# A four-layer graph network on one Trainium2 core: the planner of the order gives each DMA a time on one lane

## The chip, the cores and the metric

The kernel runs on one core of a Trainium2 chip. The core has five engines with an instruction queue each: TensorE (PE: matrix products), VectorE (DVE), ScalarE (ACT), GpSimd (POOL) and SyncE (SP, which here does nothing but issue DMAs). Each engine works its queue in the order of the program and waits on semaphores for what other engines and transfers make. The metric is the device time of one execution in microseconds.

## What is computed

128 graphs of 128 nodes with 512 features each go through four attention layers. Each is wrapped in a residual and a normalisation:

```python
x = _layernorm(x + _L0_gnn_ref(x, adj, ...))   # scores of one head; mixes x itself
x = _layernorm(x + _L1_gnn_ref(adj, x, ...))   # x @ W1 (512 x 1024), 4 heads, elu, @ W2 (1024 x 512), 1 head
x = _layernorm(x + _L2_gnn_ref(x, adj, ...))   # 8 heads of 64 columns
x = _layernorm(x + _L3_gnn_ref(x, adj, ...))   # one head; mixes x itself, elu
```

An attention layer adds a source score of a node i and a target score of a node j, takes a leaky relu, masks by the adjacency matrix, takes a softmax over one side, and multiplies by the features. In layer 1 and 2 the features are projected first. All is float32.

## The kernel before

**One graph's work.** `graph(g)` builds the list of operations of one graph. Each is an `Op`: an engine, a planned cost, a function that emits the instructions, and the buffers that it reads and writes. The helpers that matter here:

- `spread` (line 569) takes a column of scores and makes a matrix whose rows are all that column: VectorE transposes 32 x 32 blocks (L578), one DMA writes the row to a scratch in DRAM (L581, `row<-sT`), a second reads it back broadcast to 128 partitions (L585, `w<-row`). Five times a graph: three with one row, one with four, one with eight.
- `turned` (line 591) transposes n blocks of 128 x 128: VectorE transposes within 32 x 32 blocks (L596), a DMA writes the tile to scratch (L601, `scr<-w`), and a second reads it back with the blocks in their places. That read is L611 (`w<-scr`, in pieces of 128 bytes), or L606 for a matrix that is the moving side of a product. Eight times a graph: five with n = 4 and three with n = 1; L606 takes one of each, L611 the other six.
- `attend` (line 626) does the leaky relu (L635, ScalarE), mask and row minimum (L643, VectorE), the exponential (L652, ScalarE) and then `turned`. `norm` (line 667) is the normalisation; `project` (line 698) the product with a weight (L704); `mixed` (L719) the product of attention and features. `halves` (line 743) does the second product of layer 1 for two graphs together (L788) with seven block products in the place of eight.

A graph so issues 30 DMAs on SP's queue: 5 rows, 5 broadcasts, 8 writes to scratch, 8 reads back, and x, twice the adjacency matrix, and the store.

**How the order comes about.** The Python program plans before it emits anything:

1. `plan` (line 78) places one graph's operations in a period of 28 us so that, repeated for each next graph, no engine is taken twice. It uses the latencies of `LATENCY`. The result is a due time for each operation of each graph.
2. `order` (line 144) takes all operations of all graphs and of the set-up by due time and plays the run through. It keeps a clock for each engine, a time at which each operation's inputs are there (`ready`), and a time at which each buffer comes free (`released`). At each step it takes, over the engines, the operation that can start first; on one engine the oldest due one that can start at once. None may be more than 30 us (`AHEAD`) of due time ahead of the oldest that is still open. What comes out is the order of each engine's queue, and the place that each buffer takes. After an operation that starts at t, its readers may start at t + cost + `extra` + the engine's latency in `FLOW`. For SP that latency is 4.5 us, whatever else is under way.

So the planned times never reach the chip. The chip sees the order, the places and the semaphores.

**Set-up.** `at` (line 295) adds operations with due times of their own, `load` (line 307) the weights' DMAs on the queues of ACT, SP and POOL, with an `extra` of kb / 190. For w1s (16 loads) the program says 256 KB each, and 128 KB are moved; for w2s (4 loads) it says 600, and 512 are moved.

Of the kernel before, what the change touches and what calls it, by code (L numbers as in the profile page):

```python
# [29 lines left out]

PERIOD = 28.0
LATENCY = {"PE": (0.0, 0.8), "DVE": (0.15, 1.6), "ACT": (0.1, 1.6), "POOL": (0.1, 1.6), "SP": (6.8, 6.8)}
FLOW = {"PE": (0.0, 0.6), "DVE": (0.15, 0.9), "ACT": (0.1, 0.9), "POOL": (0.1, 0.9), "SP": (4.5, 4.5)}
AHEAD = 30.0
URGENCY = 0.3
BANKS = 8
# [22 lines left out]


class Op:
    def __init__(self, engine, cost, emit, ins, outs, extra, uses=()):
        self.engine, self.cost, self.emit, self.extra = engine, cost, emit, extra
        self.wait = 0
        self.ins, self.outs = ins, outs
        self.uses = list(uses)
        self.bufs = list(dict.fromkeys([*ins, *outs, *uses]))

    def done(self, reader=None, latency=None):
        own, other = (latency or LATENCY)[self.engine]  # L70
        return self.cost + self.extra + (own if reader is self.engine else other)


class Pipeline:
# [69 lines left out]
    def order(self, events):  # L144

        ops, n = [e[3] for e in events], len(events)
        ends, first, last, readers, open_uses = {}, {}, {}, {}, {}
        before, after = [0] * n, [[] for _ in ops]
        makes, coming = [[] for _ in ops], {}
        for i, op in enumerate(ops):  # L150
            need = {last[b] for b in op.ins + op.uses if b in last}
            for b in op.outs:
                need.update([last[b]] if b in last else [], readers.get(b, ()))
                if b not in first:
                    first[b] = events[i][0]
                    if b.tag != "const":
                        makes[i].append(b)
                        coming.setdefault(b.tag, []).append(i)
            need.discard(i)
            before[i] = len(need)  # L160
            for q in need:
                after[q].append(i)
            for b in op.ins + op.uses:
                readers.setdefault(b, []).append(i)
            for b in op.outs:
                last[b], readers[b] = i, []
            for b in op.bufs:
                open_uses[b] = open_uses.get(b, 0) + 1
                ends[b] = max(ends.get(b, 0.0), events[i][0] + op.done())

        free = {}
        for b, t in first.items():
            if b.tag != "const":
                places = free.setdefault(b.tag, [])
                s = next((s for s, e in enumerate(places) if e <= t), len(places))
                places[s : s + 1] = [ends[b]]
        assert len(free["ps"]) <= BANKS, "too few banks"
        free = {tag: [(0.0, s) for s in range(BANKS if tag == "ps" else len(p))] for tag, p in free.items()}
        ready, released, clock = [0.0] * n, {}, {e: 0.0 for e in FLOW}
        known = {e: [i for i in range(n) if not before[i] and ops[i].engine == e] for e in FLOW}  # L180
        issued, low, out = [False] * n, 0, []

        def start(i):
            t = max(clock[ops[i].engine], ready[i])
            for b in makes[i]:

                rank = 0
                for q in coming[b.tag]:
                    if q >= i or rank >= len(free[b.tag]):
                        break  # L190
                    rank += 1
                if rank >= len(free[b.tag]):
                    return None
                t = max(t, free[b.tag][rank][0])
            return t

        while len(out) < n:
            best = None
            for e, waiting in known.items():
                found = None  # L200
                for i in waiting:
                    if events[i][0] > events[low][0] + AHEAD and i != low:
                        break
                    t = start(i)
                    if t is not None and (found is None or t < found[0]):
                        found = (t, i)
                        if t <= clock[e]:
                            break
                if found and (best is None or found < best):
                    best = found  # L210
            t, i = best
            op = ops[i]
            known[op.engine].remove(i)
            issued[i] = True
            out.append((events[i][1], op))
            for b in makes[i]:
                b.slot = free[b.tag].pop(0)[1]
                coming[b.tag].remove(i)
            clock[op.engine] = t + op.cost
            for q in after[i]:  # L220
                ready[q] = max(ready[q], t + op.done(ops[q].engine, FLOW))
                before[q] -= 1
                if not before[q]:
                    insort(known[ops[q].engine], q)
            for b in op.bufs:
                released[b] = max(released.get(b, 0.0), t + op.done(None, FLOW))
                open_uses[b] -= 1
                if not open_uses[b] and b.slot is not None and b.tag != "const":
                    insort(free[b.tag], (released[b], b.slot))
            while low < n and issued[low]:  # L230
                low += 1
        return out
# [3 lines left out]
def tile_gat_stack(  # L236
# [55 lines left out]
    setup = []  # L292
    queue = {"SP": nc.sync, "ACT": nc.scalar, "POOL": nc.gpsimd}

    def at(t, engine, cost, emit, ins=(), outs=(), extra=0.0):
        setup.append((t, Op(engine, cost, emit, list(ins), list(outs), extra)))

    def mark():

# [256 lines left out]
    def graph(g):  # L556

        ops = []

        def op(engine, cost, emit, ins=(), outs=(), extra=0.0, uses=()):  # L560
            ops.append(Op(engine, cost, emit, list(ins), list(outs), extra, uses))

        def bank():
            return Buf("ps", [P, 512])
# [4 lines left out]
        def spread(col, nh):  # L569


            sT, row = Buf(f"sT{nh}", [P, nh, 32]), Buf(f"row{nh}", [nh, P])

            def turn():
                c, out = col(), sT.ap
                if len(c.shape) > 2:
                    out = out.rearrange("p (a b) c -> p a b c", a=c.shape[1])
                nc.vector.transpose(out, c.unsqueeze(len(c.shape)).to_broadcast([*c.shape, 32]))  # L578

            op("DVE", 0.12 + 0.033 * nh, turn, [col.buf], [sT])  # L580
            op("SP", 0.6, lambda: nc.sync.dma_start(  # L581
                out=row.ap.rearrange("h (b c) -> b h c", b=P // 32), in_=sT.ap[0:P:32]
            ), [sT], [row])
            db = Buf(f"db{nh}", [P, nh, P])
            op("SP", 0.4, lambda: nc.sync.dma_start(  # L585
                out=db.ap.rearrange("p h j -> p (h j)"),
                in_=row.ap.rearrange("h j -> (h j)").partition_broadcast(P),
            ), [row], [db], 1.0 + 0.1 * nh)
            return db

        def turned(src, n, moving=False):
# [8 lines left out]
            ), [src], [zb])  # L600
            op("SP", 0.4, lambda: nc.sync.dma_start(  # L601
                out=scr.ap, in_=zb.ap.rearrange("p b h c -> p (b h c)")
            ), [zb], [scr], 0.2 * n)
            flat = lambda: scr.ap.rearrange("p f -> (p f)")
            if moving:
                op("SP", 0.6, lambda: nc.sync.dma_start(  # L606
                    out=out.ap.rearrange("p h i -> p (h i)").rearrange("p (q e) -> p q e", q=4),
                    in_=flat().rearrange("(q p e) -> p q e", q=4, p=P),
                ), [scr], [out], 1.0)
                return out  # L610
            op("SP", 0.65, lambda: nc.sync.dma_start(  # L611
                out=out.ap.rearrange("p h (q c) -> p h q c", q=4),
                in_=flat().rearrange("(q p h c) -> p h q c", q=4, p=P, h=n),
            ), [scr], [out], 1.5)
            return out

        class Col:
            def __init__(self, buf, a, n):
                self.buf, self.a, self.n = buf, a, n
# [204 lines left out]
        def first(g):  # L824


            x0, at = Buf("x0", [P, F]), Buf("adj", [P, P], I32)
            op("SP", 0.4, lambda: nc.sync.dma_start(out=x0.ap, in_=x[g]), [], [x0], 1.0)
            op("SP", 0.4, lambda: nc.sync.dma_start(out=at.ap, in_=adj[g]), [], [at], 1.0)
            ae = Buf("ae", [P, P], I32)  # L830
            m0, m1, m2 = (Buf(f"m{k}", [P, P]) for k in range(3))
            op("POOL", 0.6, lambda: nc.gpsimd.tensor_tensor(out=ae.ap, in0=at.ap, in1=eye_i, op=ALU.add), [at], [ae])
# [72 lines left out]
        def third(g, st, xl2):  # L905
# [60 lines left out]


            at, m3 = Buf("adj", [P, P], I32), Buf("m3", [P, P])
            op("SP", 0.4, lambda: nc.sync.dma_start(out=at.ap, in_=adj[g]), [z3], [at], 1.0)
            mask(m3, at, ALU.is_equal)  # L970
            db = spread(Col(sc4, 1, 1), 1)
            pt, ri = attend(db, 0, 1, Col(sc4, 0, 1), m3, scaled=True)
# [6 lines left out]

            op("POOL", 1.3, lambda: nc.gpsimd.tensor_add(y.ap, y.ap, x3.ap), [y, x3], [y])  # L980
            norm(y, on_act=True)
            op("SP", 0.4, lambda: nc.sync.dma_start(out=out[g], in_=y.ap), [y], [], 1.0)
        if g == B:

            whole = graph(None)
# [59 lines left out]
```

## Time and profile before

| what | value |
|---|---|
| median of 3 runs | 3286.35 us (3285.72 to 3295.9) |
| the profiled execution | 3273.89 us, its span 3272.1 us |
| granted TensorE clock, mean | 0.975 |
| busy: PE, DVE, POOL, ACT | 94%, 90%, 69%, 66% of the span |
| DMA queue of SP | 598.97 MB, 74.6% of the 16 engines' span |
| packets under 512 bytes | 1311562 of 1657571 |
| stretch 600 to 1000 us: PE, DVE, POOL, ACT busy | 387.45, 370.20, 291.49, 278.45 of 400 us |
| chain that ended last | DVE 32%, PE 24%, DMA 19%, ACT 7%, POOL 6%, issue 6% |

The busy time of an engine is the union of its instructions' spans. For matmuls the ends are modelled. A table of stretches gives for each one the busy us of PE, PEld (weight loads), DVE, ACT and POOL with the number of instructions in brackets, then the granted clock, the share of the DMA engines, and GB/s. A line of waits reads: engine, tile and line that waited, what ended the wait, us in total, times, longest.

### The profile page before, as it was taken

To read this page: it belongs to the slowest core of one execution; us is meant where nothing else is said; L and a number is where in the kernel's file an instruction comes from. 1 tells how busy PE (TensorE), PEld (TensorE's weight loads), DVE (VectorE), ACT (ScalarE), POOL (GpSimd) and SP (SyncE) were. 2 spreads that over 40 slices of the span, in tenths; PEclk is the share of its full clock that TensorE was granted. 3 is DMA by queue.
4 is the path that set the end of the run, shared out by engine and by line. 5 is a ranking of instruction groups with operands and counts; after the bars stand their busy time and mean duration, and the time that the engine had idled before them with its cause. 6 is when DMAs were issued, how large, how long until landed. Compare 5 with 4: busy or idle time off the path is not lost.

```text
span 3272.1 us, 62627 instructions
## 1 busy us (share of the span) xinstructions
PE 3072.9 (94%) x14822; PEld 2483.6 (76%) x14822; DVE 2939.1 (90%) x10185; ACT 2157.7 (66%) x7427; POOL 2259.4 (69%) x3211
## 2 busy tenths in 40 slices
PE   7899999999999999999999999999999999999974
PEld 4688787778777877777888777777877777777852
DVE  6878999999989999998999998999989989999985
ACT  1346677667667666766776766767766667676764
POOL 2556777777777777766777777777777777777654
PEclk7899999999999999999999999999999999999985
DMA  4357778787777787877887777778787777787775
GB/s 114 94 129 188 191 194 193 190 201 191 196 192 193 201 189 193 200 182 185 204 194 193 195 191 200 187 193 203 191 201 190 192 193 191 194 198 195 185 180 124
DMA packets 1657571, 606.13 MB, mean 185 GB/s; under 512 B 1311562, under 2 KB 1508170, under 8 KB 1657204
## 3 DMA queue, kind: packets, MB, share of 16 engines
q1 hardware_dynamic: 1655836, 598.97, 74.6%
q8 instruction: 121, 1.98, 0.2%
q14 instruction: 246, 2.02, 0.2%
q0 software_dynamic: 576, 2.10, 0.2%
q10 hardware_dynamic: 792, 1.06, 0.1%
HBM read 374.43 MB, written 227.48 MB: 184 GB/s over the span
## 4 chain that ended last, share of the span: by engine, by line
DVE 32%; PE 24%; DMA 19%; ACT 7%; POOL 6%; issue 6%; SPq 1%; POOLq 0%; DVEq 0%; ACTq 0%
PE ps L704 14%; DVE w L643 12%; DMA w<-scr 8%; DMA scr<-w 6%; DVE w L596 6%; PE ps L788 5%; DVE st L670 3%; ACT w L652 3%; DMA w<-row 2%; ACT w L635 2%; PE ps L719 2%; DMA w<-in_x_dram 2%; PE ps L932 2%; DVE w L727 2%; PE ps L890 2%
## 5 line engine op out<-in xcount | busy, mean ns | idle before, releaser
L704 PE MATMUL ps<-w1s,w 128*128 128x258 f32 x4096 | 930.6, 385 | 21.7 <-DMA w<-scr 13.1
L652 ACT ACTIVATE w<-w,nm 128x128 f32<-128x128 f32 x1920 | 752.8, 393 | 285.4 <-DVE nm L643 265.8
L704 PEld LDWEIGHTS ps<-w1s,w 128*128 128x128 f32 x4096 | 779.0, 192 | 191.6 <-DVE z L936 18.7
L788 PE MATMUL ps<-w2s,w 128*128 128x257 f32 x3584 | 873.8, 383 | 10.0 <-POOL w L774 9.6
L643 DVE CUSTOM_DVE_ANT_0 w<-w,w 128x128 f32<-128x128 f32 x1920 | 841.2, 538 | 33.5 <-ACT w L635 16.2
L788 PEld LDWEIGHTS ps<-w2s,w 128*128 128x128 f32 x3584 | 657.3, 191 | 122.2 <-issue 27.4
L635 ACT ACTIVATE w<-w,xl 128x128 f32<-128x128 f32 x1536 | 482.1, 389 | 244.7 <-DMA w<-row 240.4
L704 PE MATMUL ps<-wha,w 128*128 128x273 f32 x2048 | 522.5, 402 | 75.6 <-DMA w<-scr 66.5
L596 DVE STREAM_TRANSPOSE w<-w 128x512 f32<-128x512 f32 (+1 forms) x1024 | 538.5, 539 | 37.1 <-POOL w L662 18.6
L704 PEld LDWEIGHTS ps<-wha,w 128*128 128x128 f32 x2048 | 379.1, 193 | 236.3 <-issue 123.1
L674 POOL TENSOR_SCALAR rd<-mv 128x1 f32<-128x1 f32 x512 | 143.0, 279 | 432.2 <-DVE mv L671 310.8
L689 ACT ACTIVATE w<-w,mr,rd 128x512 f32<-128x512 f32 x384 | 311.7, 812 | 140.1 <-POOL mr L682 75.6
L944 POOL TENSOR_TENSOR w<-z,w 128x512 f32<-128x512 f32 x128 | 151.6, 1184 | 342.7 <-DVE z L936 195.1
L675 POOL TENSOR_TENSOR rd<-rd,neghalf 128x1 f32<-128x1 f32 x512 | 345.8, 675 | 42.7
L652 ACT ACTIVATION_READ_ACCUMULATOR w<-w,nm 128x1 f32 x1920 | 362.2, 189 | 0.0
L670 DVE BATCH_NORM_STATS2 st<-w 128x6 f32<-128x512 f32 x512 | 340.3, 674 | 13.1 <-POOL w L980 9.2
L635 ACT ACTIVATE w<-w,sc 128x128 f32<-128x128 f32 x384 | 151.4, 396 | 297.2 <-DMA scr<-w 237.6
L875 POOL TENSOR_TENSOR xl<-xl,b1t 128x512 f32<-128x512 f32 x256 | 322.7, 1282 | 0.0
L719 PE MATMUL ps<-w,w 128*128 128x512 f32 x512 | 273.8, 617 | 36.5 <-DMA w<-scr 26.1
L932 PEld LDWEIGHTS ps<-xl,w 128*128 128x128 f32 x2048 | 263.0, 195 | 39.1 <-issue 11.2
L643 DVE DVE_READ_ACCUMULATOR2_ANT nm<- 128x1 f32 x1920 | 287.2, 150 | 0.0
L932 PE MATMUL ps<-xl,w 128*128 128x66 f32 x2048 | 256.1, 274 | 18.6 <-DMA w<-scr 16.5
(183 smaller groups left out, 4481.3 us busy)
## 6 DMA issues: line engine op xcount, KB each, us to landing
scr<-w SPq DMA_DIRECT2D x640, 256.0 KB
w<-scr SPq DMA_DIRECT2D x640, 256.0 KB
w<-row SPq DMA_DIRECT2D x128, 512.0 KB
w<-in_x_dram SPq DMA_DIRECT2D x128, 256.0 KB
w<-row SPq DMA_DIRECT2D x128, 256.0 KB
out_dram<-w SPq DMA_DIRECT2D x128, 256.0 KB
w<-row SPq DMA_DIRECT2D x384, 64.0 KB
scr<-w SPq DMA_DIRECT2D x384, 64.0 KB
```

The costliest lines, as they stand in the source:

```text
L596: op("DVE", 0.12 + 0.133 * n, lambda: nc.vector.transpose(zb.ap.rearrange("p b h c -> p h b c"), src.ap.rearrange("p (h b c) -> p h b c", ...
L635: nc.scalar.activation(z.ap[:, h, :], db.ap[:, h0 + h, :], AF.Prelu, bias=src(h0 + h), alpha=SLOPE)
L643: nc.vector.tensor_tensor_reduce(out=zz.ap[:, h, :].rearrange("p (b a) -> p a b", b=4), in0=z.ap[:, h, :].rearrange("p (a b) -> p a b", b= ...
L652: nc.scalar.activation(zz.ap[:, h, :], zz.ap[:, h, :], AF.Exp, bias=nm.ap[:, h : h + 1], scale=-1.0, accum_out=rs.ap[:, h : h + 1],)
L670: op("DVE", 0.6, lambda: nc.vector.bn_stats(st.ap, y.ap), [y], [st])
L675: nc.gpsimd.tensor_tensor(out=rd.ap, in0=rd.ap, in1=neghalf, op=ALU.pow)
L689: op("ACT", 0.6, lambda: nc.scalar.activation(y.ap, y.ap, AF.Identity, bias=mr.ap, scale=rd.ap), [y, rd, mr], [y])
L704: op("PE", w * 4 / 2400 + 0.006, lambda k=k: nc.tensor.matmul(px.ap[:, :w], lhsT=lhs.ap[:, k, :], rhs=wa(k, c), start=(k == 0), stop=(k == ...
L719: op("PE", width * 4 / 2400, lambda: nc.tensor.matmul(pa.ap[:, :width] if len(xv.shape) == 2 else pa.ap.rearrange("p (s c) -> p s c", s=2) ...
L788: return lambda: nc.tensor.matmul(q[b].ap[:, :C2], lhsT=x()[:, k, :], rhs=w2s[:, slot, k, :], start=(fresh and k == 0), stop=(k == 3), ski ...
L875: op("POOL", 1.3, lambda nh=nh: nc.gpsimd.tensor_add(xl.ap[:, nh, : 2 * FH], xl.ap[:, nh, : 2 * FH], b1t[:, nh * 2 * FH : (nh + 1) * 2 * F ...
L932: op("PE", 0.225, lambda u=u, h=h: nc.tensor.matmul(pa.ap[:, u * CH : (u + 1) * CH], lhsT=pt.ap[:, u, :], rhs=xl3.ap[:, h * CH : (h + 1) * ...
```

## The change

- `Op` gets a field `dma`: the time for which a transfer holds the lane. Each DMA of a graph is given one, by its kind and its n, and each load of the set-up has its kb / 190 there.
- `order` keeps one more clock, `lane`. A transfer ends at max(lane, end of its issue) + `dma`, and that is the lane's new time. Readers may start 3.2 us after it, on every engine; its buffers come free then too. The term `extra` no longer counts in `order`.
- `FLOW["SP"]` goes from 4.5 to 3.2.
- `plan` and `LATENCY` stay as they are, and so do the `extra` terms there; only set-up operations have none any more. Costs, operations and what they emit stay.

```diff
-FLOW = {..., "SP": (4.5, 4.5)}
+FLOW = {..., "SP": (3.2, 3.2)}
 ...
-    def __init__(self, engine, cost, emit, ins, outs, extra, uses=()):
+    def __init__(self, engine, cost, emit, ins, outs, extra, uses=(), dma=0.0):
+        self.dma = dma
 ...
-        ready, released, clock = [0.0] * n, {}, {e: 0.0 for e in FLOW}
+        ready, released, clock, lane = [0.0] * n, {}, {e: 0.0 for e in FLOW}, 0.0
 ...
-            clock[op.engine] = t + op.cost
+            clock[op.engine] = done = t + op.cost
+            own, other = FLOW[op.engine]
+            if op.dma:
+
+                done = lane = max(lane, done) + op.dma
+                own = other = FLOW["SP"][0]
             for q in after[i]:
-                ready[q] = max(ready[q], t + op.done(ops[q].engine, FLOW))
+                ready[q] = max(ready[q], done + (own if ops[q].engine == op.engine else other))
 ...
             for b in op.bufs:
-                released[b] = max(released.get(b, 0.0), t + op.done(None, FLOW))
+                released[b] = max(released.get(b, 0.0), done + other)
 ...
-    def at(t, engine, cost, emit, ins=(), outs=(), extra=0.0):
-        setup.append((t, Op(engine, cost, emit, list(ins), list(outs), extra)))
+    def at(t, engine, cost, emit, ins=(), outs=(), dma=0.0):
+        setup.append((t, Op(engine, cost, emit, list(ins), list(outs), 0.0, dma=dma)))
 ...
 # the time on the lane, by transfer (cost and extra unchanged)
+ L581 row<-sT                     dma=0.02 + 0.03 * nh
+ L585 w<-row        1.0 + 0.1*nh, dma=0.03 + 0.19 * nh
+ L601 scr<-w             0.2 * n, dma=0.05 + 0.17 * n
+ L606 w<-scr, moving         1.0, dma=0.27 + 0.15 * n
+ L611 w<-scr                 1.5, dma=0.415 * n
+ x in, out                   1.0, dma=0.72
+ adj (twice)                 1.0, dma=0.22
```

## The prediction

> **What bounds the kernel now.** I read the cores' view first (one core, granted clock 0.975, so no second core disturbs), then the page's busy shares, then the busy time by stretches:
>
> ```profile
> PE 3072.9 (94%) x14822; PEld 2483.6 (76%) x14822; DVE 2939.1 (90%) x10185; ACT 2157.7 (66%) x7427; POOL 2259.4 (69%) x3211
> 0.00:100.00 100.00, 74.59 (x194) 45.70 (x195) 69.36 (x258) 13.96 (x42) 28.30 (x43) 0.78 0.41 109
> 200.00:300.00 100.00, 99.04 (x490) 83.19 (x489) 81.50 (x271) 58.59 (x209) 60.66 (x76) 1.00 0.64 162
> 600.00:1000.00 400.00, 387.45 (x1909) 315.93 (x1909) 370.20 (x1299) 278.45 (x970) 291.49 (x414) 1.00 0.79 196
> ```
>
> The steady stretch sets the time. 14822 matmuls over 128 graphs are 115.8 a graph; 1909 of them in 400 us are 16.5 graphs, so a graph takes 24.3 us. TensorE is busy 97% of it, VectorE 93%, the DMA engines 79%. The fill and the tail lose some 160 us (1071 matmuls in the first 300 us are 9.2 graphs, or 224 us at the steady rate), and I expect little change there.
>
> How much is there to win? From runs of matmuls without a break in the chain that ended last:
>
> ```profile
> 1515.78 3.22 PE ps L704 x14
> 1519.00 1.73 PE ps L932 x16
> 1522.53 0.86 PE ps L719 x2
> 1552.99 6.96 PE ps L704 x32
> 1561.25 1.78 PE ps L890 x16
> ```
>
> At these rates a graph needs 6.96 (layer 1 projection) + 28 x 0.2175 = 6.09 (layer 2, from a run of 8 in 1.74 us that the chain has at 186.8 us) + 16 x 0.23 = 3.68 (layer 2 heads' projection on wha) + 3 x 0.86 + 1.73 + 1.78 + 0.11 = 22.9 us. Against 24.3 that leaves 1.4 us a graph: 0.8 us is open idle time (busy sums to 2610 of 2700 us from 300 to 3000), the rest is hidden in matmuls that the model shows as busy.
>
> The waits of TensorE from 300 to 3000 us, and the DMA issue before one of them:
>
> ```profile
> PE ps L704 <- DMA w<-scr: 65.4, 83, 3.0
> PE ps L844 <- POOL w L732: 7.5, 14, 2.0
> PE ps L890 <- DMA w<-scr: 1.7, 4, 0.6
> 1507.45 7.39 SPq L611 DMA_DIRECT2D w<-scr  x3
> 1507.45 7.38 DMA w<-scr
> ```
>
> Columns of a wait: total us, times, longest. So 67 of the 90 us of open idle are waits for one kind of transfer, the read back of a transposed tile (L611). The last two lines show why some are late: three such reads went out in one burst, SP stood in their issue for 7.39 us, and the chain charges 7.38 us to the transfer. The order was laid down with 0.65 + 1.5 + 4.5 = 6.65 us for every such read, alone or third in line. The same chain charges 6.45 and 6.10 us to the next two. I also matched the trace's packets to the issues by size and order: from 300 to 3000 us the last packet of a 2048-packet read lands 3.3 us after its issue at the tenth percentile, 4.75 at the median, 6.1 at the ninetieth. A transfer's time depends on what stands ahead of it, and the kernel's order does not know it.
>
> **What the Trainium skill says.** "DMA: Bandwidth & Descriptors", section Queues, rings and completion order: the queue of one issuing engine is one ring on each DMA engine, consumed in ring order. The burst of three agrees, and so one lane is a fair picture. The same page, Issuing engines are not separate DMA queues: loads from other engines share the 16 DMA engines; the change puts the weights from ACT and POOL on the lane too, and the GB/s row (114 in the first slice) shows no second set of engines. "TensorE: Matmul & The Clock Gate", HAM oscillation: idle gaps of more than about 3.4 us halve the clock. The trace agrees once in the steady part: after 3.0 us of idle at 1540 us, clock 0.50 from 1540.2 to 1543.4 us. "Perfetto Trace Analysis", Identifying the Most-Contended Engine: matmul busy time is a poor measure of the room left; hence the working by rates above.
>
> **The change, part by part.** It adds and removes no instruction; every duration stays, and only the order in each engine's queue and the buffers' places move.
>
> *The read L611 (four of n = 4, two of n = 1 a graph).* Planned from 6.65 to 0.65 + 1.66 + 3.2 = 5.51 us alone, and 1.66 more for each one ahead: third in a burst from 6.65 to some 7.5 (3 x 1.66 of lane, less the 1.3 by which its own issue is later). Against the packets, the old figure is 3.3 us over a lone read (tenth percentile) and 0.5 over the late ones (ninetieth); the new one is 2.2 over the first and 1.4 over the second.
>
> *The other transfers, planned alone, before to after:* score row to DRAM (L581) 5.1 to 3.85; broadcast of one row (L585) 6.0 to 3.82, of four 6.3 to 4.39, of eight 6.7 to 5.15; tile to scratch (L601) 5.7 to 4.33; L606 of four 6.1 to 4.67. Last packets land (median, from issue) at 1.2, 2.9, 3.5, 5.0, 3.2 and 2.9 us. The new figures are nearer and mostly still long.
>
> *What the lane adds.* By the new figures a graph holds it for: rows 0.55, broadcasts 3.00, writes 4.31, reads 8.76, loads and store 1.88; sum 18.5 us of 24.3, or 76%, against the page's 79% DMA share. The sum of squares is 19.5 us2 a graph; if issues came at random, the mean queue would be 19.5 / (2 x 24.3 x 0.24) = 1.7 us. SP spaces them, so I estimate 1.0 to 1.7 us. Then a read averages 6.5 to 7.2 us in the new plan against 6.65: the mean margin is kept, and it moves to where the queue is. That is my reason for a gain: a matmul that needs the last of a burst is put later and another graph's work before it. The cover is there: VectorE, ScalarE and GpSimd hold work of several graphs, and the queue of TensorE holds 28 layer 2 matmuls that can go between.
>
> *Size.* Unknown from a page, so bounded. Best: all 67 us of waits for L611 and L606. Worst: the planned time of a lone read falls by 1.14 us; if every one of the 83 waits grew by that, +95 us. I take half the waits back, -34 us: the queue's own noise, SP's stall in issue (the plan has 0.65 us for it) and VectorE at 93% keep the other half.
>
> *Set-up.* Loads lose their term of kb / 190 without a queue and take the same time on the lane: 16 of 1.35 us and 4 of 3.2 us are 34 us of lane. In the profile VectorE waits 11.0 us for the first w1s weights, since the old order believes them there after some 6 us; a later place for them lets work of the first graphs go ahead. I take half, -5.5 us; bounds -11 and +11 (the lane holds w1s too long: 256 KB is planned, 128 KB is moved).
>
> *Buffers.* Numbers of places follow from the other latency table, which stays; release in the plan moves with the same figures. Nothing by itself.
>
> Sum: -34 - 5.5 = -39.5 us. The profiled execution took 3273.89 us (span 3272.1 and 1.8 around it) and becomes 3234; the median of the runs, 12.5 above it, goes from 3286.35 to 3247.
>
> **The rivals.**
> *More than half.* All 67 us go, the hidden loss falls with the open idle (0.6 of 0.8, so about 43 us of the steady part), and set-up gives 11: -121, or 3165 us. For it: 1.4 us a graph are off the floor. Against: VectorE at 370 of 400 us would then be next at 22.5 us.
> *No change.* VectorE's queue decides: its planned costs are short (L953 takes 658 ns, the planner has 0.2 us for its group), and every engine waits for it in turn. For it: DVE has 32% of the chain, DMA 19%. Then 3286 us.
> *Slower.* One mechanism: the plan trusts lone transfers too early. A graph has thirteen chains of two transfers in a row (five broadcasts, eight transposes), and each is planned 2.5 to 3.7 us shorter alone (5.1 + 6.0 to 3.85 + 3.82 for one row's broadcast). Where upstream work runs late on the chip, that length was the cover. It decides from the point where the plan's mean queue is under 1.14 us for the reads: then TensorE takes the wha projection earlier than now. Half of the bound of 95 us: +47, or 3333 us. For it: the waits of PE are already on this read, with 6.1 to 7.4 us since its issue.
> *It does nothing:* only if the order came out equal; every time in the plan moves, so I give it no chance of its own.
>
> **How the numbers follow.** Half back 0.50, more 0.12, no change 0.13, slower 0.25. A measurement of this kernel tells 0.3% (10 us) from no change. The likeliest case has its own range of 3206 (waits gone, no more) to 3280; a little of it falls within 10 us. Faster 0.61, same 0.14, slower 0.25. The range for 8 in 10 runs from 3180 to 3333: it leaves out the better part of the second case and the half of the slower case that is worse than its middle.
>
> **What would show it.** Right: waits of PE L704 for w<-scr from 300 to 3000 us near 33 instead of 65; more than 1909 matmuls (about 1933) in 400 us; the same counts and mean durations in every group. The queue step is wrong if bursts of three L611 are as long and PE's waits for them do not fall; the set-up step if the first 300 us hold no more than 1071 matmuls. The prediction fails if the waits move to VectorE or to `w<-row`, or if PE's waits for w<-scr grow in number: then the margin, not the queue, was what the old figures gave.

## The result and the profile after

The changed kernel takes 3208.66 us (median of 4 runs, 3205.95 to 3213.19) against 3286.03 us for the kernel before in the same measurement: a ratio of 0.9762, 95% interval 0.9737 to 0.9786, or 77 us less. Forecast were 39 us less, 3247 us. The time lies in the range that was given, and the direction is right; the gain is 1.97 times the forecast. Two later measurements of the same kernel beside the kernel before, on chips 7 and 11 of the record, gave 0.9702 and 0.9757.

The page of the changed kernel (busy us, share of the span, instructions), and its busy time by stretches (PE, PEld, DVE, ACT, POOL, then clock, DMA share and GB/s):

```profile
PE 3050.0 (95%) x14822; PEld 2483.6 (77%) x14822; DVE 2967.3 (92%) x10185; ACT 2172.0 (68%) x7427; POOL 2285.5 (71%) x3211
0.00:100.00 100.00, 76.61 (x213) 47.29 (x214) 73.21 (x270) 15.07 (x46) 35.84 (x46) 0.83 0.41 116
200.00:300.00 100.00, 100.00 (x502) 84.27 (x501) 80.45 (x286) 65.44 (x234) 62.30 (x80) 1.00 0.70 177
600.00:1000.00 400.00, 391.00 (x1935) 321.54 (x1934) 382.58 (x1318) 285.04 (x977) 298.73 (x418) 1.00 0.80 197
```

The counts of instructions are the same as before, as they must be when only the order moved. In the same 400 us there are 1935 matmuls for 1909, so a graph takes 23.9 us for 24.3. The granted clock is 1.00 in both. VectorE's 10185 instructions now take 2967 us of busy time for 2939, so durations did not quite stay; the last section has one reason.

The waits of TensorE in the changed kernel from 300 to 3000 us (the numbers of lines are six higher after the change: L710, L850, L738 and L641 were L704, L844, L732 and L635):

```profile
PE ps L850 <- POOL w L738: 58.4, 101, 2.2
PE ps L794 <- POOL w L780: 2.4, 3, 1.3
PE ps L710 <- DMA w<-scr: 0.3, 1, 0.3
```

The 65.4 us of waits for w<-scr are gone, all but 0.3. In their place stands one wait that was 7.5 us: the transpose of a mask (L850) for the mask itself, which GpSimd makes (L738). The open idle time of TensorE falls only from 89.7 to 61.8 us. ScalarE shows the other half of the change. Its two largest waits of before, from 300 to 3000 us, then its largest of after and the two of before again:

```profile
ACT w L635 <- DMA scr<-w: 234.4, 154, 3.8
ACT w L635 <- DMA w<-row: 226.0, 158, 4.2
```

```profile
ACT w L658 <- DVE nm L649: 301.4, 388, 4.3
ACT w L641 <- DMA w<-row: 47.9, 64, 2.4
ACT w L641 <- DMA scr<-w: 4.1, 7, 1.2
```

L635 (after: L641) reads a broadcast row and writes a new tile. Its wait for w<-row is for its input. Its wait for scr<-w cannot be: it reads nothing of that transfer. It is the wait for the place in which its output goes, from which an earlier transfer still reads. The two together were 460 us and are 52 us now. ScalarE's idle time as a whole fell only from 824 to 781 us, since other waits grew: for VectorE (L658, before L652) from 197 to 301, for GpSimd (L695, before L689) from 102 to 262. Summed over a trace by what ended each wait, from 300 to 3000 us: for DMA, TensorE waited 67.9 us before and 0.3 after, VectorE 43.5 and 8.5; all idle time of VectorE fell from 207 to 131 us.

**Where the time went.** The two profiled executions are 3273.89 and 3213.19 us, 61 apart. Counting matmuls in order of time, the 1158th (ten graphs' worth) starts at 317.0 us before and at 302.0 after; the 14000th at 3016.9 and 2958.2. So 15 us were gained in the fill, 44 in the steady part, and 2 in the tail. The other 17 of the 77 us are in the runs' medians alone: the profiled execution of before was 12 us below its median, that of after 5 us above. In which part of the run those 17 lie is not known. In the steady part, over the seven stretches from 300 to 3000 us, TensorE was busy 2610.3 us for 12860 matmuls and then 2638.2 us for 13075. By the matmul that is 3.4 ns less, 2.2 of it open idle and 1.2 hidden in the busy time; over 13075 matmuls, 29 and 16 us.

### The profile page after: what moved, and what is told of

It reads as the page before. It is cut to its first block, busy times and chain, and to the rows that moved or that the text cites. A ratio compares the mean times of both kernels' runs of the same rounds, so it can differ in the third digit from the quotient of the medians.

```text
span 3211.2 us, 62683 instructions
## 1 busy us (share of the span) xinstructions
PE 3050.0 (95%) x14822; PEld 2483.6 (77%) x14822; DVE 2967.3 (92%) x10185; ACT 2172.0 (68%) x7427; POOL 2285.5 (71%) x3211
## 3 DMA queue, kind: packets, MB, share of 16 engines
q8 instruction: 120, 1.97, 0.3%
## 5 line engine op out<-in xcount | busy, mean ns | idle before, releaser
L658 ACT ACTIVATE w<-w,nm 128x128 f32<-128x128 f32 x1920 | 754.2, 394 | 389.5 <-DVE nm L649 347.3
L710 PE MATMUL ps<-w1s,w 128*128 128x258 f32 x4096 | 940.3, 383 | 7.1 <-DMA w<-scr 7.1
L710 PEld LDWEIGHTS ps<-w1s,w 128*128 128x128 f32 x4096 | 780.7, 191 | 176.8 <-issue 30.0
L649 DVE CUSTOM_DVE_ANT_0 w<-w,w 128x128 f32<-128x128 f32 x1920 | 853.6, 545 | 14.4 <-ACT w L641 12.1
L710 PE MATMUL ps<-wha,w 128*128 128x273 f32 x2048 | 518.4, 397 | 4.7 <-DMA w<-scr 4.2
L695 ACT ACTIVATE w<-w,mr,rd 128x512 f32<-128x512 f32 x384 | 311.5, 812 | 298.8 <-POOL mr L688 207.2
L641 ACT ACTIVATE w<-w,xl 128x128 f32<-128x128 f32 x1536 | 480.4, 389 | 35.0 <-DMA w<-row 32.4
L710 PEld LDWEIGHTS ps<-wha,w 128*128 128x128 f32 x2048 | 389.2, 195 | 134.9 <-issue 35.6
L680 POOL TENSOR_SCALAR rd<-mv 128x1 f32<-128x1 f32 x512 | 153.3, 299 | 341.2 <-DVE mv L677 184.5
L658 ACT ACTIVATION_READ_ACCUMULATOR w<-w,nm 128x1 f32 x1920 | 361.4, 188 | 0.0
L717 ACT COPY xl<-ps 128x258 f32<-128x258 f32 (+1 forms) x640 | 226.4, 363 | 153.5 <-PE ps L710 152.7
L649 DVE DVE_READ_ACCUMULATOR2_ANT nm<- 128x1 f32 x1920 | 288.2, 150 | 0.0
```

Of the source, the lines that this page charges most:

```text
L641: nc.scalar.activation(z.ap[:, h, :], db.ap[:, h0 + h, :], AF.Prelu, bias=src(h0 + h), alpha=SLOPE)
L649: nc.vector.tensor_tensor_reduce(out=zz.ap[:, h, :].rearrange("p (b a) -> p a b", b=4), in0=z.ap[:, h, :].rearrange("p (a b) -> p a b", b= ...
L658: nc.scalar.activation(zz.ap[:, h, :], zz.ap[:, h, :], AF.Exp, bias=nm.ap[:, h : h + 1], scale=-1.0, accum_out=rs.ap[:, h : h + 1],)
L695: op("ACT", 0.6, lambda: nc.scalar.activation(y.ap, y.ap, AF.Identity, bias=mr.ap, scale=rd.ap), [y, rd, mr], [y])
L710: op("PE", w * 4 / 2400 + 0.006, lambda k=k: nc.tensor.matmul(px.ap[:, :w], lhsT=lhs.ap[:, k, :], rhs=wa(k, c), start=(k == 0), stop=(k == ...
```

## The experiments

Each kernel ran beside the kernel before on its chip; the ratios below are to that. The kernel before itself differed from chip to chip (3287 to 3315 us), so kernels are best compared where they shared one. The chips are named by their numbers in the record; the first and the last group ran on the same one.

| kernel | us | ratio to before, 95% interval | a graph in the plan, us |
|---|---|---|---|
| chip 11: e1_no_queue | 3303.45 | 1.0059 (1.0036 to 1.0081) | 22.95 |
| e2_flat_shorter | 3253.40 | 0.9897 (0.9878 to 0.9917) | 23.02 |
| e3_old_figures_and_queue | 3375.95 | 1.0270 (1.0254 to 1.0287) | 23.61 |
| e4_setup_alone | 3287.69 | 1.0004 (0.9992 to 1.0016) | 23.20 |
| chip 9: e5_mean_without_queue | 3289.96 | 0.9962 (0.9948 to 0.9976) | 23.02 |
| e6_lane_33 | 3222.05 | 0.9762 (0.9743 to 0.9781) | 23.02 |
| e7_lane_28 | 3247.20 | 0.9840 (0.9819 to 0.9861) | 22.96 |
| e8_pool_cost | 3242.02 | 0.9827 (0.9803 to 0.9850) | 23.06 |
| chip 6: e9_late_transpose | 3254.58 | 0.9806 (0.9785 to 0.9828) | 23.00 |
| e10_late_transpose_4 | 3273.32 | 0.9862 (0.9841 to 0.9884) | 22.99 |
| e11_graphs_alone | 3207.07 | 0.9661 (0.9637 to 0.9685) | 23.02 |
| e12_old_figures_queue_35 | 3246.48 | 0.9783 (0.9757 to 0.9809) | 23.22 |
| chip 7: e13_changed_again | 3217.26 | 0.9702 (0.9682 to 0.9721) | 23.02 |
| e14_graphs_alone_again | 3206.24 | 0.9675 (0.9656 to 0.9695) | 23.02 |
| e15_flat_38 | 3299.10 | 0.9951 (0.9934 to 0.9969) | 23.02 |
| chip 11 again: e16_lane_for_release | 3227.58 | 0.9818 (0.9783 to 0.9854) | 23.00 |
| e17_lane_for_readers | 3206.36 | 0.9749 (0.9714 to 0.9785) | 23.02 |
| e18_changed_third | 3207.94 | 0.9757 (0.9728 to 0.9787) | 23.02 |

The last column is no time of the chip. It is the rate at which the Python program believes that its own order will run, and it is 23.20 us for the kernel before. It serves to compare orders that are equally full by their own account. By the same account the lane holds one of the four large reads (L611, n = 4) back by 0.90 us on average, 1.85 us at the ninetieth percentile.

**Queue or length?** Two things changed at once: transfers are planned shorter, and they queue. Theory Q says that knowing the queue makes the gain; theory T, that shorter transfers let the plan fill TensorE better.

The changed kernel without the queue:

```diff
-                done = lane = max(lane, done) + op.dma
+                done += op.dma
```

> The changed kernel with the lane forgotten after each transfer: every DMA keeps its new time by kind and the 3.2 us, but nothing stands in a queue in the plan. Theory Q (the plan's knowledge of the queue makes the gain): reads in a burst are believed there too soon; TensorE's waits for w<-scr from 300 to 3000 us come back to 65 us or more, and the time is 3250 us or above, perhaps above 3286. Theory T (the gain is that transfers are planned shorter, so that the plan fills TensorE; the queue is not needed): 3195 to 3220 us, waits for w<-scr under 15 us.

It is 0.6% slower than the kernel before, though its plan is the fullest of all. T is refuted in its plain form; Q's time came, and by a way that it did not name. TensorE waits little for w<-scr (13.6 us), and most for the mask of GpSimd. Its largest wait, and those of VectorE in this kernel, from 300 to 3000 us:

```profile
PE ps L850 <- POOL w L738: 96.9, 97, 2.0
DVE w L649 <- DMA scr<-w: 116.6, 56, 3.8
DVE w L744 <- DMA w<-in_x_dram: 49.5, 69, 2.6
DVE w L903 <- ACT w L902: 18.2, 32, 1.5
```

L649 is the mask and minimum, which reads ScalarE's tile and a mask. Its only tie to a scr<-w transfer is the place of its output. The plan believes the place free too early, and the chip's VectorE stands in front of a place that is still being read, with all that is behind it in the queue. The transfer itself is not too short in the plan: the writes behind these 56 waits end 3.1 us (median) after their issue begins, and the plan has 3.8 or 4.3. They are issued late. For 55 of the 56, their own issue or one of the four ahead of it on SP's queue took over 1.5 us, where the plan has 0.65 at most; of all writes to scratch that holds for 268 of 877. In the plan only the queue on the lane makes such a write late. How these waits reach TensorE was not followed.

One number changed in the kernel before, the flat 4.5 us of SP to 4.1, and in a later run to 3.8:

```diff
-FLOW = {..., "SP": (4.5, 4.5)}
+FLOW = {..., "SP": (4.1, 4.1)}    # e15: (3.8, 3.8)
```

> The kernel before with one number changed: SP's flat figure 4.1 in the place of 4.5 us, no lane, the set-up's old terms. In the program's own plan TensorE is then as full as in the changed kernel (99.7% of 600 to 2600 us against 99.0% before). Theory Q: within 20 us of before (3266 to 3306), waits of TensorE for w<-scr at 60 us or more. Theory T: 3200 to 3230 us, those waits under 15 us.

> The kernel before with a flat 3.8 us for SP and no lane; the program's own plan has 23.02 us a graph, as at 4.1 us and as in the changed kernel. If a flat figure's best is near 1%: a ratio of 0.988 to 1.002, as less cover costs on the chip what a fuller plan gains. If the flat figure could do what the lane does: under 0.980.

4.1 us gain 1.0%, between what both theories said: T has a part in it. The waits of TensorE for w<-scr fall even here to 5.5 us, and the wait for GpSimd rises to 70.4. So those waits, which I took for the trace of the queue, go with the length too. But 3.8 us, with an equally full plan, gives half of that back, on another chip. VectorE's waits in that kernel, same stretch:

```profile
DVE w L643 <- DMA scr<-w: 135.6, 53, 4.7
DVE w L693 <- POOL rd L675: 27.5, 55, 0.8
DVE w L596 <- POOL w L662: 19.5, 56, 0.4
```

It is the same wait for a place as without the queue, and again all 53 have an issue of over 1.5 us at them or just ahead. Of the flat figures tried the best is near 1%.

The old figures with the queue added on top, as an edit of the changed kernel:

```diff
-FLOW = {..., "SP": (3.2, 3.2)}
+FLOW = {..., "SP": (4.5, 4.5)}    # e12: (3.5, 3.5)
 ...
+            done += op.extra
             if op.dma:
-                done = lane = max(lane, done) + op.dma
-                own = other = FLOW["SP"][0]
+                wait = max(0.0, lane - (t + op.cost))
+                lane = max(lane, t + op.cost) + op.dma
+                done += wait
```

> The kernel before with the old figures (cost, extra, 4.5 us) and the lane's waiting time added on top: only the queue is new. The program's own plan gets 2.5% longer, TensorE 97.4% full in it. Theory Q: TensorE's waits for w<-scr fall under 20 us and the time is at or below before, 3220 to 3286 us. Theory T: longer planned transfers cost time, 3290 to 3350 us.

At 4.5 us it is 2.7% slower: planned this long, transfers empty the plan, by 1.8% by its own account. The rest is not told; the last section has a candidate. That is T's outcome. But it changes the plan's fill along with the queue. So the two were told apart at an equal fill. With the new figures by kind, the lane was taken out and its mean put in its place:

```diff
-FLOW = {..., "SP": (3.2, 3.2)}
+FLOW = {..., "SP": (4.1, 4.1)}
 ...
-                done = lane = max(lane, done) + op.dma
+                done += op.dma
```

> The changed kernel without the lane, and with 4.1 us in the place of 3.2: each DMA keeps its time by kind, and every one gets the same 0.9 us more that the lane adds to a read on average in the program's own plan. That plan has the same rate as the changed kernel's (a graph in 23.02 us, TensorE 99.7% full from 600 to 2600 us). Theory Q (which transfer waits in the queue matters, beyond the mean): 3240 to 3290 us. Theory T (only how long transfers are planned on the mean, and so how full the plan is, matters): 3200 to 3225 us, as the changed kernel.

0.9962, where the changed kernel with 3.3 us in the place of 3.2 has 0.9762 on the same chip and the same rate in the plan. With the old figures and 3.5 us, so that the plan is as full as before, the queue was put in:

> The old figures with the lane's waiting time on top, as in the run with 4.5 us, but with 3.5 us for SP, so that the program's own plan has the rate of the plan before (23.22 us a graph against 23.20, TensorE 98.8% full against 99.0%). Theory Q: faster than before by 1% to 2.5%, as knowing the queue was worth 2% at an equal rate of the plan with the new figures by kind. Theory that queue and figures by kind only work together: within 0.5% of before.

0.9783. So at an equal fill of the plan the queue is worth 2.0% with the new figures and 2.2% with the old ones. Q holds, and it needs no help from the figures by kind.

Which waits go with that? From 300 to 3000 us, all waits of VectorE and ScalarE that a scr<-w ended (waits for a place, as scr<-w writes nothing that they read), and those of ScalarE that a w<-row ended (waits for input):

| kernels, by fill of the plan | for places, us | for rows, us | ratio |
|---|---|---|---|
| 23.0: e11 and e14, set-up off the lane | 5.8, 7.3 | 91, 106 | 0.9661, 0.9675 |
| 23.0: changed, three times | 6.5 to 8.8 | 48 to 85 | 0.9702 to 0.9762 |
| 23.0: e6 | 7.6 | 47 | 0.9762 |
| 23.0: e17 | 14.5 | 58 | 0.9749 |
| 23.0: e16 | 55.5 | 142 | 0.9818 |
| 23.0: e2 | 90.7 | 28 | 0.9897 |
| 23.0: e5 | 125.6 | 128 | 0.9962 |
| 23.0: e15 | 158.3 | 30 | 0.9951 |
| 23.2: e12 | 64.3 | 242 | 0.9783 |
| 23.2: before | 244.6 | 226 | 1 |

The time goes with the waits for places and not with those for rows: e12 gains 2.2% with more of the latter than before. That is an order among kernels and not an experiment, since none changed the places alone; and places are not all, for e8 to e10 below have 10 to 37 us and lie at 0.981 to 0.986.

**Readers or release?** The lane is used twice: it says when a transfer's readers may start, and when its buffers come free. The prediction had said that the second does nothing by itself. With `mean` for the time by kind and 4.1 us:

```diff
+            freed = done + other
+            if op.dma:
+                mean = done + op.dma + 4.1
+                lane = max(lane, done) + op.dma
+                real = lane + 3.2
+                done, freed = mean, real     # e17: real, mean
+                own = other = 0.0
 ...
-                released[b] = max(released.get(b, 0.0), done + other)
+                released[b] = max(released.get(b, 0.0), freed)
```

> Readers of a transfer start by its time by kind and 4.1 us, as in the run with the mean and no queue; only the release of the buffers follows the lane and 3.2 us. The program's own plan has 23.00 us a graph. If the release is what the queue is known for: a ratio of 0.970 to 0.980 to before, as the changed kernel, and waits of VectorE and ScalarE for scr<-w near nothing. If the readers are: 0.990 to 1.000, as without the queue.

> The reverse: readers follow the lane and 3.2 us, the buffers are released by the time by kind and 4.1 us. The program's own plan has 23.02 us a graph. If the readers' start is what counts, as the prediction held: 0.970 to 0.980. If the release is: 0.990 to 1.000, with waits of VectorE or ScalarE for scr<-w of over 80 us from 300 to 3000 us.

> The changed kernel beside the two runs before: a ratio of 0.968 to 0.978.

The readers alone give all of it (0.9749 against 0.9757 beside it). The release alone gives the larger part (0.9818; the same figures with no queue at all, e5, had 0.9962 on another chip). Neither of the two theories of the expectations is right as it stood: the two uses are not two shares of a sum. The readers' run has its buffers released by the same mean as e5 and yet hardly a wait for places. So a release by the mean does not by itself make those waits. The waits of VectorE in it, and e5's wait for a place:

```profile
DVE w L605 <- POOL w L671: 34.1, 94, 1.8
DVE w L702 <- POOL rd L684: 25.5, 55, 0.6
DVE w L854 <- DMA scr<-w: 14.0, 16, 1.8
```

```profile
DVE w L851 <- DMA scr<-w: 80.5, 52, 3.5
```

Why one of the two is nearly enough was not tried further.

**How fine is the figure?** The changed kernel with 3.3 and with 2.8 us:

```diff
-FLOW = {..., "SP": (3.2, 3.2)}
+FLOW = {..., "SP": (3.3, 3.3)}    # e7: (2.8, 2.8)
```

> The changed kernel with 3.3 in the place of 3.2 us after the lane. The program's own plan has the same rate (23.02 us). It asks how much one order differs from another at nearly the same figures. If the order's luck is small: 3200 to 3220 us. If it is large, the difference is over 20 us, and single comparisons of this size say little of a theory.

> The changed kernel with 2.8 us after the lane: TensorE 100% full in the program's own plan from 600 to 2600 us (a graph in 22.96 us), each transfer planned 0.4 us shorter. Theory T alone: faster than the changed kernel, 3190 to 3208 us. Theory of cover (the planned length hides work that runs late on the chip; the kernel with no queue lost to it): 3225 to 3270 us, waits of VectorE and TensorE for DMA above 30 us from 300 to 3000 us.

3.3 us give the same ratio to the last digit. One pair does not measure the luck of an order, though: 0.05 us on each operation of GpSimd (e8 below, on the same chip) cost 0.65%, with the plan 0.2% less full. Differences of that size between two orders may be luck; 2%, found twice, is well above it. 2.8 us are 0.8% worse than 3.3 with a fuller plan, as the theory of cover said: TensorE waits 37 us for w<-scr again, VectorE 81 us for x (L744) and 23 us for a place at L733, and ScalarE 178 us for rows.

**The set-up.** The lane for its loads alone, and for the graphs' transfers alone:

```diff
-            if op.dma:
+            if op.dma and events[i][1] < 0:      # e4: set-up; all else by the old figure
 ...
+            if op.dma and events[i][1] < 0:      # e11, e14: set-up by the old figure
+                done += op.dma
+                own, other = (4.5, 4.5) if op.engine == "SP" else FLOW[op.engine]
+            elif op.dma:
+                done = lane = max(lane, done) + op.dma
```

> The kernel before with the lane for the set-up's loads alone; the graphs' transfers have the old figures. By the profiles 15 of the 61 us between the two profiled executions were gained before the 1158th matmul. If the set-up's loads did that: 10 to 17 us less than before, 3269 to 3276 us, the 1158th matmul at 302 us in the place of 317. If the graphs' own transfers did it: within 6 us of before.

> The changed kernel with the set-up's loads planned as before (cost, kb / 190 and 4.5 us, off the lane) and the graphs' transfers on the lane. With it, the set-up's part of the change is told in the company of the rest. If the loads on the lane gave the 15 us before the 1158th matmul: that matmul is back at 317 us and the time 3220 to 3228. If the graphs' transfers gave them: within 8 us of the changed kernel, 3201 to 3217.

> The changed kernel itself, beside the next two on one chip. By its first measurement a ratio of 0.976 to before; if kernels with little waiting for DMA are less touched by a chip on which the kernel before is slow, 0.966 to 0.972.

> The graphs' transfers on the lane and the set-up's loads as before. If the loads on the lane cost something: 0.5% to 1% under the changed kernel in the same call. If they do nothing and the earlier ratio of 0.966 came from the chip: within 0.3% of the changed kernel.

Alone, the loads do nothing for the time: 1.0004. Their 1158th matmul starts at 309.3 us, 8 earlier than before, and the steady part takes it back. With the graphs' transfers alone the 1158th matmul starts at 304.0 and 302.9 us, against 302.0 in the changed kernel (301.6 to 302.0 in its three measurements). So either part alone shortens the fill, by 8 and by 13 to 14 of the 15 us, and beside the graphs' transfers the loads add 1 or 2. Leaving the loads off the lane is even better by 11 us on the same chip (0.9675 against 0.9702), and that kernel has the lowest ratio of all in both of its measurements. The difference does not arise in the fill: the 14000th matmul starts at 2962.1 us in the changed kernel there and at 2951.5 in this one, after a start 1.2 us later. The loads only set another order going, and what in it is better was not told; 0.3% may be luck.

**The wait that is left.** TensorE's 58 us for the mask of GpSimd were attacked twice: GpSimd planned 0.05 us dearer for each operation, and the one edge from the mask to its transpose planned 2 or 4 us longer.

```diff
-            clock[op.engine] = done = t + op.cost
+            clock[op.engine] = done = t + op.cost + (0.05 if op.engine == "POOL" else 0.0)
```

```diff
+            ops[-1].late = 2.0     # e10: 4.0; of the transpose of m2, added to its ready time in order
```

> The changed kernel with 0.05 us more for each operation of GpSimd in the run that lays down the order. In the changed kernel TensorE waits 58 us for the masks of GpSimd (L738 ahead of L850), whose queue runs later than planned; no other wait is near it. If that lateness is GpSimd's planned cost: waits of L850 under 40 us and 3180 to 3200 us. If it comes from what GpSimd itself waits for (VectorE's sums, L677): the wait stays at 50 to 70 us and the time at 3200 to 3220 us.

> The changed kernel with 2.0 us more, in the run that lays down the order, between the mask m2 of GpSimd (L738) and the transpose of it on TensorE (L850); its result is needed only after the layer 1 projection. It asks what the one wait left on TensorE is worth. If TensorE is still the bound: waits of L850 under 20 us and 3165 to 3195 us on a chip where the changed kernel takes 3209. If VectorE is the bound now (it idles 131 us of 2700): waits of L850 fall and the time stays at 3198 to 3218 us.

> As the run with 2.0 us, with 4.0 us on the same edge; the program's own plan has nearly the same rate (22.99 us a graph against 23.00). If TensorE is the bound, waits of L850 at nearly nothing and the same time as with 2.0 us or less, 3160 to 3195 us; if VectorE is the bound, 3198 to 3218 us.

All three have a higher ratio than the changed kernel; the first shared a chip with e6 (0.9762), the other two with e11 (0.9661). Dearer operations raised the wait to 71.7 us. With 2 us on the edge the waits of TensorE are:

```profile
PE ps L850 <- POOL w L738: 14.4, 19, 1.1
PE ps L710 <- DMA w<-scr: 14.0, 25, 1.3
PE ps L725 <- DMA w<-scr: 8.4, 15, 1.0
PE ps L939 <- DVE w L983: 8.2, 15, 1.2
PE ps L939 <- DMA w<-scr: 7.2, 10, 2.1
```

The one wait went as intended, and its 44 us came back as small ones and more: TensorE's idle time is 78 us for 62, VectorE's 152 for 131. With 4 us it is gone, and TensorE waits 39.5 us for VectorE at L939 instead. So these runs do not say which engine is the bound; they say that this wait was not worth its 58 us. A wait that ends at GpSimd is there because GpSimd's queue waits for others first: each of the 101 waits from 300 to 3000 us, followed back through GpSimd's queue, comes to the first step of a normalisation (L680) that had waited for another engine, 49 times for VectorE's sums (L677) and 52 times for ScalarE, nearly always its copy of a projection (L717).

## Why the prediction was right and where it failed

**The step that failed** is the steady part of the sum: "half of the waits back, -34 us", with "Buffers: nothing by itself" beside it. It read TensorE's waits for one transfer as the whole account. The steady part gave 44 us, by other terms: those waits all went, 51 us of a wait for GpSimd stand in their place, and the loss hidden in busy time, which the sum left out, shrank too. And the buffers, put at nothing because the other latency table stays, are where most of the gain can come from: with the release alone on the lane the ratio is 0.9818, and 0.9962 without (e5, on another chip).

*The bound and the room.* The steady stretch does set the time, a graph going from 24.3 towards the 22.9 us of the estimate, and the tail changed little. Whether TensorE or VectorE (96% busy now) is the bound after the change, no run says. The fill was said to change little and gave 15 us.

*The waits for w<-scr are the queue's.* Half right. They went, and knowing the queue is worth 2% at an equal fill. But a flat figure 0.4 us shorter takes most of these waits away as well. What goes with the time beyond that lies elsewhere: in the waits of ScalarE and VectorE for places, which the prediction did not list, since it read the waits of TensorE alone. Its own sign for this step, the bursts of three reads, does not decide either: such reads one behind another on SP's queue fell from 107 cases to 53 from 300 to 3000 us, as long each (5.9 and 5.8 us at the median), but there are 54 without the queue too (e1, e5).

*Half of the waits come back: -34 us.* This is the term that was mis-sized. It should have been -45 us in the profiled pair: none of the 67 us were kept by "the queue's own noise, SP's stall in issue and VectorE at 93%". Instead 51 us of another wait appeared (L850 for GpSimd), 29 us of open idle were left as the net gain, and the hidden loss, which the sum left out and only the rival "more than half" had, gave 16 more. That the stretch from 600 to 1000 us has 1935 matmuls, where the prediction's sign was about 1933, is luck of the stretch: the five after it gained 28 to 51 each. It is luck too that the time lies beside the 3206 us that the prediction gave to "waits gone, no more".

*The reading of transfer times.* It compared the plan with the last packets. Readers wait for the semaphore, and in the same trace its last update comes 0.5 to 0.7 us later for the large reads: 3.85 us after the issue begins at the tenth percentile, 5.3 at the median, 6.8 at the ninetieth. So the old 6.65 us did not cover the late ones. The broadcasts come at 3.8, 4.5 and 5.4 us at the median for one, four and eight rows; against 3.82, 4.39 and 5.15, the new figures without the queue are not "mostly still long" for them.

*Set-up: -5.5 us.* The step failed in the time: the loads on the lane gave nothing (1.0004). Its sign came true, with 1151 matmuls in the first 300 us for 1071, but does not tell the loads from the rest: with the loads alone there are 1112, with the graphs' transfers alone 1143. For those the sum had no term in the fill.

*The step from the profiled execution to the median.* 12.5 us were carried over unchanged. The changed kernel's profiled execution was 5 us above its median, so 17 of the 77 us come in here; without them the gain is 61 for 39.5.

*Buffers: nothing by itself.* Wrong. Release by the lane alone is worth most of the gain. It is not needed, though, when the readers follow the lane, so why the places come free in time there stays open.

*The clock.* The prediction saw one stretch of half clock in the steady part, after 3.0 us of idle, and took it for agreement with a limit of more than 3.4. There are two between 300 and 3000 us, and the other follows 2.04 us of idle that ended at 378.0 us:

```profile
379.60:383.00 3.40, 3.40 (x9) 2.49 (x8) 3.40 (x9) 1.31 (x3) 3.21 (x5) 0.50 0.92 205
```

So in this trace shorter gaps went with a halved clock too. No term of the sum rests on it.

*The rivals.* The slower one has the right mechanism: cover lost by planning transfers too short is real, and e1, e7 and e15 show it. Its deciding point was wrong: a mean queue of 1.14 us for the reads. The plan's mean is 0.90 us, under it, and the kernel is faster by 2.4%. The mean is not what counts, as the run with the mean and no queue shows (0.4%); each transfer's own place in the queue does. "No change", with VectorE's queue deciding, did not come true: the time fell by 2.4% and VectorE's idle time with it.

## What to carry to other kernels

Where a program lays down queues by playing the run through, a shared resource has to be in the play, not its mean: at an equal fill of the plan the lane was worth 2%, and its mean 0.4%. A transfer believed done too early is not only read too early, its buffer is handed out too early as well, and that wait shows up on an engine that has nothing to do with the transfer, so look at the waits of all engines for a DMA that they don't read. And one remaining wait of the busiest engine is no promise of its length: here the orders that took 44 or all of the 58 us away were slower.

## What was not expected of the hardware

The kernel before took 3287, 3301, 3315, 3313 and 3287 us on chips 11, 9, 6, 7 and 11 again, a spread of 0.9% between chips. On the two chips where the changed kernel ran beside it, 7 and 11, it took 3217 and 3208 us against 3313 and 3287. So it differs less from chip to chip, on this small count, and part of the ratio is the chip's. In the run with the old figures and the queue VectorE was "busy" more than in any other, with fewer matmuls done:

```profile
600.00:1000.00 400.00, 378.22 (x1844) 308.54 (x1845) 391.81 (x1248) 269.41 (x930) 281.49 (x401) 0.99 0.76 188
```

391.81 of 400 us, at 1248 instructions for 1318 in the changed kernel. The same instruction, mask and minimum, before (L643) and in this run (L650):

```profile
L643 DVE CUSTOM_DVE_ANT_0 w<-w,w 128x128 f32<-128x128 f32 x1920 | 841.2, 538 | 33.5 <-ACT w L635 16.2 <-PE ps L719 14.0 <-DMA scr<-w 2.7
L650 DVE CUSTOM_DVE_ANT_0 w<-w,w 128x128 f32<-128x128 f32 x1920 | 980.7, 619 | 10.2 <-ACT w L642 10.0 <-PE ps L726 0.2
```

The mean grew from 538 to 619 ns, but the median did not: 379 and 381. What grew is the number of those that take over 1 us, some 1.4 us at the median: 247 of 1920 before, 262 in the changed kernel, 426 here. In each of these traces every one of them overlaps an elementwise instruction of GpSimd of over 1 us and ends within 0.26 us of its end; of the 1437 before that take at most 0.5 us, 60 overlap one. So by these records VectorE stands until GpSimd is done and is counted as busy; the order decides how often the two meet, and VectorE's busy share is no measure of how near it is to its limit.
